# An SSM convolution with a 16-expert feed-forward on one core: the first convolution kernels computed on VectorE alone, the later ones tied to given heads

## The chip, the core and the metric

The kernel runs on one core of a Trainium2 chip. The core has a TensorE for matrix products, a VectorE (DVE in the profile) and a ScalarE (ACT) for element-wise work, a GpSimd (POOL), and a SyncE (SP) that here only issues DMA transfers. Sixteen DMA engines move data between DRAM and the on-chip memory. Each engine has its own instruction queue and takes it in order; engines wait for each other through semaphores. The metric is the device time of one execution in microseconds; lower is better.

## What is computed

The input `x` has 128 batch rows, 32 heads and 512 positions. Cut to what matters, the reference is:

```python
# per head: a convolution kernel from a diagonal state space model
K = 2 * einsum('hn,hnl->hl', Ct, exp(dtA[:, :, None] * arange(512))).real
y = causal_convolution(x, K) + x * D          # by FFT in the reference
y = y * (arange(512) < length[:, None])       # each batch row has its length
# per token (128 * 32 tokens of 512 values): mixture of experts
scores = sigmoid(y @ gate_w.T) + bias         # 16 experts, the best 4 weighted
out = sum over the 4 experts of w * (silu(y @ Wg.T) * (y @ Wu.T)) @ Wd.T
out = out + (silu(y @ Sg.T) * (y @ Su.T)) @ Sd.T     # shared expert
return x + out
```

## The kernel before, in words

The work runs in four stages. Everything up to the third is put in order by a scheduler that goes over the program with a priority by the order in which it was written and gives an idle engine the first instruction that is ready, so an engine may run ahead of the written order, but never out of the order in which the scheduler laid it down.

**Start.** SyncE loads the small parameters, then the first blocks of the transposed input (`load_xt`) and the shared expert's weights. GpSimd fills constants: `dsk` (line 127), `run_on` and `run_e` (223 to 228), `f_r` and `f_i` (290, 291), the masks and counters. The convolution kernels `K` are made in chunks of *pairs* of heads, `CHUNKS = ((0, 2), (2, 4), (6, 4), (10, 6))`: first pair and number of pairs, so the first chunk makes heads 0 to 3. For a chunk, `waves` (line 295) computes angle, sine, cosine and magnitude over a table of 48 columns for each pair: `reduce_angle` (line 242) is a chain of six VectorE instructions, `exp_parts` (line 250) one of twelve that depend on each other. `kernels` (line 367) multiplies these into two small factors, of which TensorE forms the products `pk` (line 394); VectorE adds the skip term into `krow` (line 402), which is written to a scratch tensor `kd` in DRAM. `kernel_strip` (line 413) reads it back, shifted by one for each partition, as the Toeplitz matrix `strip` of a block of four heads: 1 MB, for block 0 in four pieces of 256 KB. In `waves` and `kernels` half of the element-wise products are given to GpSimd (lines 309, 349 to 351, 374, 382, 386, 389).

Beside the kernels, VectorE ranks the batch rows by length (lines 430 to 512): `to_rank`, `to_row`, `within`, and what only later stages need (`by_rank`, `reach`, `k_u`, `unit_rows`).

**Convolution.** Eight blocks `tb` of four heads, `h = 4 * tb + q`. `convolve` (line 515) makes four products of 512, 384, 256 and 128 columns into `py` (line 520), VectorE masks them into `yb` (line 527), TensorE transposes by `to_rank` into `pt` (line 530), and ScalarE copies to `yT` in `store` (line 531). At heads 0, 2 and 5 (`chunk_at`) the program makes a further chunk of kernels, waves and products together; at the first head of a block it issues the strip of the block after. At a block's end `yb` goes to DRAM on ScalarE's queue, the block's gate scores are made (`gates`, `sums`), and after each second block `route` picks the experts on VectorE. GpSimd's queue issues copies of `x` to the output, DRAM to DRAM, 1 MB for a part of four heads, tied to the last head of a block: `COPIES = {2: (0,), 3: (1,), 4: (2,), 5: (3,), 6: (4, 5), 7: (6, 7)}`.

**Shared expert** (`unit_step`): eight units of 512 tokens; the results are added onto the output rows by indirect DMAs from GpSimd (line 953). In this stage the slots of the expert tiles are worked out as well, and the first seven experts' weights loaded. From here on the order is written out by hand.

**Expert tiles** (`turn_of`): about 134 tiles of 128 tokens each: gather, transpose, two layers of products (lines 1054 and 1080), and an indirect DMA that adds onto the output (line 1090).

Of the kernel before, what the change touches and what calls it, by code (L numbers as in the profile page):

```python
# [28 lines left out]
F32 = mybir.dt.float32  # L29
BF16 = mybir.dt.bfloat16  # L30
F16 = mybir.dt.float16
I32 = mybir.dt.int32
# [6 lines left out]
P = 128  # L39
# [4 lines left out]
HB = 4  # L44
# [10 lines left out]
ONE_HOTS = 8  # L55
AHEAD = 4
# [19 lines left out]
def ssm_moe_kernel(  # L76
# [50 lines left out]
    nc.gpsimd.memset(dsk, 0.0)  # L127
# [21 lines left out]
    def load_xt(tb):  # L149
        t = xp.tile([P, KT, HB, P], F32, tag="x", name=f"xt{tb}")  # L150
        nc.sync.dma_start(out=t, in_=x_t[tb])
        return t

# [69 lines left out]
    nc.gpsimd.memset(run_on, 1.0)  # L223
    nc.gpsimd.memset(run_on[:, :, 0:1], 0.0)

    run_e = const.tile([P, RB * HB, E], F32, tag="run_e", name="run_e")
    nc.gpsimd.memset(run_e, 1.0)
    nc.gpsimd.memset(run_e[:, :, 0:1], 0.0)

    def floor_div(out_, in_, by):  # L230

        nc.vector.tensor_scalar(
            out_, in_, 1.0 / by, -(by - 1) / (2.0 * by), ALU.mult, ALU.add
        )
        nc.vector.tensor_scalar(out_, out_, ROUND, None, ALU.add)
        nc.vector.tensor_scalar(out_, out_, ROUND, None, ALU.subtract)

# [35 lines left out]
    CHUNKS = ((0, 2), (2, 4), (6, 4), (10, 6))  # L273
# [16 lines left out]
    nc.gpsimd.memset(f_r, 0.0)  # L290
    nc.gpsimd.memset(f_i, 0.0)
# [3 lines left out]
    def waves(c0, n, lead):  # L295


        w = lead + n * NX
        v, r, k, q = (wide(t, w) for t in ("wv", "wr", "wk", "wq"))
        s, mag = wide("ws", w, I32), wide("wm", w)  # L300

        def pairs(t):
            return t[:, lead:].rearrange("p (c x) -> p c x", x=NX)

        by_l = lab.unsqueeze(1).to_broadcast([P, n, NX])
        nc.vector.tensor_mul(
            pairs(r), by_l, dta_i[:, c0 : c0 + n].unsqueeze(2).to_broadcast([P, n, NX])
        )
        nc.gpsimd.tensor_mul(
            pairs(v), by_l, dta_r[:, c0 : c0 + n].unsqueeze(2).to_broadcast([P, n, NX])  # L310
        )
        if lead:
            nc.vector.tensor_copy(r[:, :lead], dta_i)
            nc.vector.tensor_copy(v[:, :lead], dta_r)
        reduce_angle(r, k)
        nc.vector.scalar_tensor_tensor(k, r, -1.0, r, ALU.mult, ALU.max)
        nc.scalar.activation(k, k, AF.Sin, bias=half_pi, scale=-1.0)
        half = None
        if lead:
            half = ptile("half")  # L320
            nc.scalar.activation(half, r[:, :lead], AF.Sin, scale=0.5)
        nc.scalar.activation(r, r, AF.Sin)
        exp_parts(v, q, wide("we", w), s)
        s = s.bitcast(F32)
        nc.vector.scalar_tensor_tensor(mag, q, 1.0, s, ALU.add, ALU.mult)
        return tuple(pairs(t) for t in (mag, k, r)), (mag, q, s, r, half)
# [22 lines left out]
    nc.gpsimd.tensor_mul(m0, nar, nar)  # L349
    nc.gpsimd.tensor_mul(m1, aim, aim)  # L350
    nc.gpsimd.tensor_add(m0, m0, m1)
# [15 lines left out]
    def kernels(c0, n, mag, cos, sin):  # L367

        cs = slice(c0, c0 + n)

        for j in range(2):
            rows = slice(j * N, (j + 1) * N)
            nc.vector.tensor_mul(f_r[rows, cs, j, :], cos[rows, :, LA:], mag[rows, :, LA:])
            nc.gpsimd.tensor_mul(f_i[rows, cs, j, :], sin[rows, :, LA:], mag[rows, :, LA:])
# [7 lines left out]
        nc.gpsimd.tensor_mul(e_i, sin[:, :, :LA], mag[:, :, :LA])  # L382
# [3 lines left out]
        nc.gpsimd.tensor_mul(g_t, e_i, by_i)  # L386
        nc.vector.tensor_add(g_r, g_r, g_t)
        nc.vector.tensor_mul(g_i, e_r, by_i)
        nc.gpsimd.tensor_mul(e_i, e_i, by_r)
# [12 lines left out]
        nc.vector.tensor_add(  # L402
# [7 lines left out]
        for h in range(2 * c0, 2 * (c0 + n)):  # L410
            kd_of[h] = kd[h - 2 * c0 : h - 2 * c0 + 1, :]

    def kernel_strip(tb):
        s = ks1.tile([P, HB, L], F32, tag="strip", name=f"strip{tb}", bufs=2)

        each = 1 if tb == 0 else HB
        for q in range(0, HB, each):
            kd = kd_of[tb * HB + q]
            nc.sync.dma_start(
                out=s[:, q : q + each, :],  # L420
                in_=bass.AP(kd.tensor, kd.offset, [[1, P], [PAD + L, each], [1, L]]),
            )
        strip[tb] = s

    kernels(*CHUNKS[0], *first)
    kernel_strip(0)


    len_col = const.tile([P, 1], F32, tag="len_col", name="len_col")
    nc.vector.tensor_copy(len_col, len_col_i)  # L430
    key_row = const.tile([P, B], F32, tag="key_row", name="key_row")
    nc.vector.tensor_copy(key_row, len_row_i)
    key_col = const.tile([P, 1], F32, tag="key_col", name="key_col")
    for key, raw, own in ((key_row, key_row, cpos), (key_col, len_col, ppos)):
        nc.vector.tensor_scalar(key, raw, 0.0, float(L), ALU.max, ALU.min)
        if key is key_col:
            num_len = const.tile([P, 2], F16, tag="num_len", name="num_len")
            nc.vector.tensor_copy(num_len[:, 0:1], ppos)
            nc.vector.tensor_copy(num_len[:, 1:2], key)
        nc.vector.scalar_tensor_tensor(key, key, float(P), own, ALU.mult, ALU.subtract)  # L440
# [14 lines left out]
    to_rank_h = const.tile([P, P], F16, tag="to_rank_h", name="to_rank_h")  # L455
    nc.vector.tensor_copy(to_rank_h, to_rank)

    by_rank_ps = ps_m.tile([P, 2], F32, tag="m", name="by_rank_ps")
    nc.tensor.matmul(by_rank_ps, lhsT=to_rank_h, rhs=num_len, start=True, stop=True)
    by_rank = const.tile([P, 2], F32, tag="by_rank", name="by_rank")  # L460
    nc.vector.tensor_copy(by_rank, by_rank_ps)


    reach = const.tile([P, KT], BF16, tag="reach", name="reach")
    nc.vector.memset(reach, 1.0)
    for n in range(1, KT):
        nc.vector.tensor_scalar(
            reach[:, n : n + 1], by_rank[:, 1:2], float(n * P), None, ALU.is_gt
        )

    unit = const.tile([P, NU], BF16, tag="unit", name="unit")
    nc.vector.tensor_scalar(unit, upos, 0.0, None, ALU.is_equal)
    reach_sum = const.tile([P, 1], F32, tag="reach_sum", name="reach_sum")
    nc.vector.tensor_reduce(reach_sum, reach, AX.X, ALU.add)
    reach_b = const.tile([P, 1], BF16, tag="reach_b", name="reach_b")
    nc.vector.tensor_copy(reach_b, reach_sum)
    k_u_ps = ps_m.tile([1, NU], F32, tag="m", name="k_u_ps")
    nc.tensor.matmul(k_u_ps, lhsT=reach_b, rhs=unit, start=True, stop=True)
    k_u = const.tile([1, NU], I32, tag="k_u", name="k_u")
    nc.vector.tensor_copy(k_u, k_u_ps)  # L480


    div = const.tile([P, 2], F32, tag="div", name="div")
    mod = const.tile([P, 1], F32, tag="mod", name="mod")
    floor_div(div[:, 0:1], rank, UB)
    floor_div(div[:, 1:2], ppos, UB)
    nc.vector.scalar_tensor_tensor(mod, div[:, 0:1], -float(UB), rank, ALU.mult, ALU.add)
    same_mod = const.tile([P, P], F16, tag="same_mod", name="same_mod")
    nc.vector.tensor_scalar(same_mod, pmod, mod, None, ALU.is_equal)
    row_u = const.tile([P, NU], F16, tag="row_u", name="row_u")  # L490
    nc.vector.tensor_scalar(
        row_u, cpos[:, :NU], div[:, 0:1], ppos, ALU.is_equal, ALU.mult
    )
    row_ps = ps_m.tile([P, NU], F32, tag="m", name="row_ps")
    nc.tensor.matmul(row_ps, lhsT=same_mod, rhs=row_u, start=True, stop=True)
    part = const.tile([P, TU // P], F32, tag="part", name="part")
    nc.vector.tensor_scalar(
        part, cpos[:, : TU // P], float(P // UB), div[:, 1:2], ALU.mult, ALU.add
    )
    unit_rows = const.tile([P, NU, TU // P], I32, tag="unit_rows", name="unit_rows")  # L500
    nc.vector.scalar_tensor_tensor(
        unit_rows,
        row_ps.unsqueeze(2).to_broadcast([P, NU, TU // P]),
        float(H),
        part.unsqueeze(1).to_broadcast([P, NU, TU // P]),
        ALU.mult,
        ALU.add,
    )
# [3 lines left out]
    nc.vector.tensor_scalar(within, lpos, len_col, None, ALU.is_lt)  # L512
# [328 lines left out]
    def dep(of, on, why):  # L841
        tc.add_manual_dep(of.ins, on.ins.name, SYNC, reason=why)

# [4 lines left out]
    COPIES = {2: (0,), 3: (1,), 4: (2,), 5: (3,), 6: (4, 5), 7: (6, 7)}  # L848

    chunk_at = {0: CHUNKS[1], 2: CHUNKS[2], HB + 1: CHUNKS[3]}  # L850
    for tb in range(NB):
        yb = yp.tile([P, HB, L], F32, tag="yb", name=f"yb{tb}")
        x_next = load_xt(tb + 1) if tb + 1 < NB else None
        for q in range(HB):
            turned = convolve(tb, q, xb, yb)
            if tb * HB + q in chunk_at:
                c0, n = chunk_at[tb * HB + q]
                kernels(c0, n, *waves(c0, n, 0)[0])
            if q == 0 and tb + 1 < NB:
                kernel_strip(tb + 1)  # L860
# [355 lines left out]
```

## Time and profile before

| | us |
|---|---|
| time, median of 3 runs | 943.94 (941.65 to 944.29) |
| the profiled execution, its own time | 942.44 |
| its span, first to last instruction | 940.7 |

| stage of the profiled execution | from, us | to, us | TensorE busy, us |
|---|---|---|---|
| start, up to the first convolution product | 0 | 27.6 | 1.7 |
| convolution, 8 blocks | 27.6 | 146.3 | 109.0 |
| shared expert | 146.3 | 298.0 | 147.9 |
| expert tiles | 298.0 | 940.7 | 624.6 |

The stages are read from the timeline: the first product of line 520 starts at 27.59, the first of line 929 (shared expert) at 146.31, and the first of line 1054 (expert tiles) at 298.12. The busy time of each is taken from the windows by stage.

A row of the timeline gives start, duration, engine, line of the program, operation, the tiles it writes and reads, its shape and how many instructions were merged; in brackets stands how long its engine was idle before it and what released it. A row of the waits gives total time, number of times and the longest. `SPq` and `ACTq` are the instructions that issue DMA transfers on those engines.

### The profile page before, as it was taken

What the parts mean: (1) busy time and instruction counts of PE and PEld (TensorE: products, weight loads), DVE (VectorE), ACT (ScalarE), POOL (GpSimd) and SP (SyncE); (2) the same over time, 40 slices, a digit from 0 to 9 for tenths busy, and PEclk for the clock granted to TensorE, in tenths of its full rate; (3) what the DMA queues carried; (4) which work ended last, traced back from release to release, by engine and by line L of the source; (5) the groups of instructions that cost most, each with busy time, mean ns of one, the idle gap of its engine ahead of it and who ended that gap; (6) DMA issues with size and microseconds to landing.
All of it is one profiled execution on the core that took longest, in us unless ns stands there. A gap on an engine that the chain in (4) does not pass through costs nothing.

```text
span 940.7 us, 14509 instructions
## 1 busy us (share of the span) xinstructions
PE 883.1 (94%) x2960; PEld 442.0 (47%) x2960; DVE 409.3 (44%) x1406; ACT 190.0 (20%) x375; POOL 422.7 (45%) x376
## 2 busy tenths in 40 slices
PE   0799997999999999999999999999999999999993
PEld 0455553444544444454444444444444444444441
DVE  7954555486950233433343334333433233344331
ACT  0122221111222122211222122212211111222220
POOL 4210000222456455655565456645655545566553
PEclk9999999999999999999999999999999999999997
DMA  4378873276769756776577567756766556667664
GB/s 163 108 253 290 293 275 137 30 249 132 184 96 233 198 111 115 138 170 116 110 135 181 114 115 126 130 101 110 134 113 114 100 106 109 109 130 138 118 114 83
DMA packets 54673, 135.95 MB, mean 145 GB/s; under 512 B 12400, under 2 KB 12560, under 8 KB 50960
## 3 DMA queue, kind: packets, MB, share of 16 engines
q0 software_dynamic: 36256, 89.77, 50.6%
q1 hardware_dynamic: 14064, 36.15, 11.3%
q10 hardware_dynamic: 4224, 8.39, 2.3%
q8 instruction: 71, 1.16, 0.5%
q14 instruction: 58, 0.48, 0.1%
HBM read 288.08 MB, written 60.64 MB: 371 GB/s over the span
## 4 chain that ended last, share of the span: by engine, by line
PE 66%; issue 1%; SPq 0%; POOL 0%; DVE 0%; ACT 0%; POOLq 0%
PE g L1054 34%; PE o L1080 24%; PE m L1022 4%; PE u L1072 3%; PE o L944 1%; POOL out L1090 0%; SPq L1157 0%; POOL yg L894 0%; SPq L1105 0%; SPq L1140 0%; SPq L1141 0%; DVE zt L1066 0%; SPq L1142 0%; ACT sgt L1065 0%; SPq L880 0%
## 5 line engine op out<-in xcount | busy, mean ns | idle before, releaser
L1054 PE MATMUL g<-store,yt 128*128 x742 | 343.0, 596 | 1.8 <-issue 1.5
L1090 POOL DMA_INDIRECT out<-ob,put x134 | 211.3, 1577 | 242.6 <-DVE junk L1029 214.4
L1080 PE MATMUL o<-store,zT 128*128 x536 | 252.2, 593 | 0.1
L1066 DVE SCALAR_TENSOR_TENSOR zt<-g,wt,sgt 128x256 f32<-128x256 f32 x135 | 65.3, 484 | 306.7 <-ACT sgt L1065 306.7
L1054 PEld LDWEIGHTS g<-store,yt 128*128 128x128 f32 x742 | 130.3, 190 | 118.7 <-issue 117.4
L1080 PEld LDWEIGHTS o<-store,zT 128*128 128x128 f32 x536 | 101.4, 190 | 129.3 <-issue 124.6
L894 POOL DMA_INDIRECT yg<-y_rows,get x140 | 138.1, 987 | 42.7 <-issue 31.7
L1089 DVE COPY ob<-o 128x512 f32<-128x512 f32 x134 | 92.7, 692 | 109.7 <-PE o L1080 101.6
L1028 ACT COPY yt<-m 128x512 f32<-128x512 f32 x136 | 79.7, 586 | 227.7 <-PE m L1022 219.3
L1065 ACT ACTIVATE sgt<-g 128x256 f32<-128x256 f32 x135 | 51.9, 384 | 268.2 <-PE g L1054 267.4
L953 POOL DMA_INDIRECT out<-ob,unit_rows x32 | 50.2, 1568 | 98.8 <-ACT ob L951 93.1
L520 PE MATMUL py<-strip,xt 128*128 128x512 f32 (+3 forms) x256 | 79.0, 447 | 7.9 <-DMA strip<-kd 7.9
L1022 PEld LDWEIGHTS m<-ident,yg 128*128 128x128 f32 x373 | 48.6, 141 | 73.1 <-issue 73.0
L1022 PE MATMUL m<-ident,yg 128*128 128x128 f32 x373 | 63.1, 273 | 1.3 <-issue 1.0
L944 PE MATMUL o<-store,z 128*128 128x512 f32 x128 | 57.7, 597 | 1.2 <-ACT yt L1028 1.2
L1075 DVE COPY zT<-u 128x256 f32<-128x256 f32 x134 | 56.3, 420 | 0.7 <-PE u L1072 0.7
L520 PEld LDWEIGHTS py<-strip,xt 128*128 128x128 f32 x256 | 42.5, 195 | 25.3 <-issue 12.3
L1072 PE MATMUL u<-ident,zt 128*128 128x128 f32 x268 | 51.2, 273 | 0.6 <-DVE zt L1066 0.6
L929 PE MATMUL g<-store 128*128 128x512 f32 x92 | 43.0, 602 | 3.1 <-issue 2.5
L865 POOL DMA_DIRECT2D out<-in_x x8 | 4.4, 558 | 88.3 <-ACT store L531 88.3
L929 PE MATMUL u<-store 128*128 128x512 f32 x92 | 42.2, 593 | 0.0
L809 DVE TENSOR_SCALAR cols<-tpos_h,stl,tok 128x143 f16<-128x143 f16 x128 | 41.8, 331 | 0.0
(272 smaller groups left out, 499.0 us busy)
## 6 DMA issues: line engine op xcount, KB each, us to landing
store<-in_w_all SPq DMA_DIRECT2D x143, 1536.0 KB
xt<-in_x_t SPq DMA_DIRECT2D x8, 1024.0 KB
y_rows<-yb ACTq DMA_DIRECT2D x8, 1024.0 KB
out<-in_x POOLq DMA_DIRECT2D x8, 1024.0 KB, 9.0
strip<-kd SPq DMA_DIRECT2D x7, 1024.0 KB
yg<-y_rows,get POOLq DMA_INDIRECT x140, 4.3
out<-ob,put POOLq DMA_INDIRECT x134, 4.8
strip<-kd SPq DMA_DIRECT2D x4, 256.0 KB
```

The lines of the kernel that those rows point to most:

```text
L520: nc.tensor.matmul(py[:, : L - jt * P], lhsT=xt[:, jt, q, :], rhs=strip[tb][:, q, jt * P :], start=(jt == 0), stop=(jt == KT - 1),)
L894: nc.gpsimd.indirect_dma_start(out=at(yg, t), out_offset=None, in_=y_rows[:, :], in_offset=bass.IndirectOffsetOnAxis(ap=made["get"][:, t : ...
L929: nc.tensor.matmul(ps[it], lhsT=w_sh[:, c0 : c0 + P], rhs=yT[:, u, kt, :, :].rearrange("p h b -> p (h b)"), start=(kt == KT - n), stop=(kt ...
L944: nc.tensor.matmul(po, lhsT=at(zu, u)[:, it, q * P : (q + 1) * P], rhs=w_sh[:, c0 : c0 + L], start=(it == 0), stop=(it == IT - 1),)
L1022: nc.tensor.transpose(pt[:, q, :], at(yg, t)[:, q * P : (q + 1) * P], ident)
L1028: nc.scalar.copy(at(yt, t), pt)
L1054: mm = nc.tensor.matmul(pgu, lhsT=at(yt, t)[:, q, :], rhs=ring_flat[:, bass.ds(w0s[t] + q * 2 * I, 2 * I)], start=(q == KT - n), stop=(q = ...
L1066: nc.vector.scalar_tensor_tensor(at(zs, t), pgu[:, I:], at(wts, t), sg, ALU.mult, ALU.mult)
L1072: nc.tensor.transpose(at(p_z, t)[:, it, :], at(zs, t)[:, it * P : (it + 1) * P], ident)
L1080: mm = nc.tensor.matmul(po, lhsT=at(zts, t)[:, it, :], rhs=ring_flat[:, bass.ds(w0s[t] + WD + it * L, L)], start=(it == 0), stop=(it == IT ...
L1089: nc.vector.tensor_copy(ob, po)
L1090: add = nc.gpsimd.indirect_dma_start(out=out, out_offset=bass.IndirectOffsetOnAxis(ap=made["put"][:, t : t + 1], axis=0), in_=ob, in_offse ...
```

## The change

Six edits belong together.

1. The fills of `dsk`, `run_on`, `run_e`, `f_r` and `f_i` go from GpSimd to VectorE.
2. For the first chunk, the products that GpSimd made in `waves` and `kernels`, and the three of lines 349 to 351, go to VectorE. Later chunks keep them on GpSimd.
3. A helper `behind` ties an instruction to the first chunk's `krow`. It is put on the first instructions of the ranking, on `within`, and on the first instruction of later chunks' waves on both engines. What else ranks and only serves later stages moves into a function `ranks`, called when block 2 begins.
4. `keep_warm` puts 16 TensorE products of bf16 ones, 128x512 each, behind the first chunk's `krow`.
5. The chunks become five, and waves and products are written at different heads; a strip is issued as soon as its chunk is made, and no earlier than one block ahead.
6. The copies of `x` begin one block later, and four of the eight are issued behind the last block.

```diff
-    nc.gpsimd.memset(dsk, 0.0)
+    nc.vector.memset(dsk, 0.0)
...
-    nc.gpsimd.memset(f_r, 0.0)
-    nc.gpsimd.memset(f_i, 0.0)
+    nc.vector.memset(f_r, 0.0)
+    nc.vector.memset(f_i, 0.0)
...
-    CHUNKS = ((0, 2), (2, 4), (6, 4), (10, 6))
+    CHUNKS = ((0, 2), (2, 2), (4, 4), (8, 4), (12, 4))
...
-        nc.vector.tensor_mul(
+        first_op = nc.vector.tensor_mul(
             pairs(r), by_l, dta_i[...]
         )
-        nc.gpsimd.tensor_mul(
+        if c0:
+            behind(first_op)
+        first_op = (nc.gpsimd if c0 else nc.vector).tensor_mul(
             pairs(v), by_l, dta_r[...]
         )
+        if c0:
+            behind(first_op)
...
+        other = nc.gpsimd if c0 else nc.vector
...
-            nc.gpsimd.tensor_mul(f_i[rows, cs, j, :], sin[rows, :, LA:], mag[rows, :, LA:])
+            other.tensor_mul(f_i[rows, cs, j, :], sin[rows, :, LA:], mag[rows, :, LA:])
...
-    kernels(*CHUNKS[0], *first)
+    def keep_warm(on):
+        warm = ps_u.tile([P, KT, P], F32, tag="u", name="warm")
+        for n in range(WARM):                      # WARM = 16
+            mm = nc.tensor.matmul(
+                warm,
+                lhsT=ones,
+                rhs=ones.unsqueeze(1).to_broadcast([P, KT, P]),
+                start=True,
+                stop=True,
+            )
+            dep(mm, on, "behind the first kernels")
+
+    chunk0 = kernels(*CHUNKS[0], *first)
     kernel_strip(0)
+    keep_warm(chunk0)
+
+    def behind(op):
+        dep(op, chunk0, "later in VectorE's order")
...
-    COPIES = {2: (0,), 3: (1,), 4: (2,), 5: (3,), 6: (4, 5), 7: (6, 7)}
-    chunk_at = {0: CHUNKS[1], 2: CHUNKS[2], HB + 1: CHUNKS[3]}
+    COPIES = {3: (0,), 4: (1,), 5: (2,), 6: (3,), 7: (4, 5, 6, 7)}
+    waves_at = {0: CHUNKS[1], 2: CHUNKS[2], 7: CHUNKS[3], 12: CHUNKS[4]}
+    kernels_at = {0: CHUNKS[1], 5: CHUNKS[2], 10: CHUNKS[3], 16: CHUNKS[4]}
+    made_waves, strips = {}, [1]
     for tb in range(NB):
+        if tb == 2:
+            by_rank, reach, k_u, unit_rows = ranks()
...
             turned = convolve(tb, q, xb, yb)
-            if tb * HB + q in chunk_at:
-                c0, n = chunk_at[tb * HB + q]
-                kernels(c0, n, *waves(c0, n, 0)[0])
-            if q == 0 and tb + 1 < NB:
-                kernel_strip(tb + 1)
+            h = tb * HB + q
+            if h in waves_at:
+                made_waves[waves_at[h]] = waves(*waves_at[h], 0)[0]
+            if h in kernels_at:
+                kernels(*kernels_at[h], *made_waves[kernels_at[h]])
+            if strips[-1] in (tb, tb + 1) and strips[-1] < NB and strips[-1] * HB in kd_of:
+                kernel_strip(strips[-1])
+                strips.append(strips[-1] + 1)
```

## The prediction

> **What bounds the kernel now.** I first read the page's engine table and its slices, then the windows by stage, then TensorE's waits, and last the timeline of the first 50 us. The page:
>
> ```profile
> PE 883.1 (94%) x2960; PEld 442.0 (47%) x2960; DVE 409.3 (44%) x1406; ACT 190.0 (20%) x375; POOL 422.7 (45%) x376
> ...
> PE   0799997999999999999999999999999999999993
> ```
>
> TensorE is busy all the time but for the first slice (23.5 us each) and a little of the second and seventh. The expert stages, from 146.3 us on, have TensorE as their limit (772.5 us busy in 794.4 us), and the change touches nothing in them. So only two things can move the end: when the first convolution product starts (27.59 us), and what TensorE idles between it and 146.3 us: 118.7 us with 109.0 busy, 9.7 idle. The waits of TensorE in that stage say who causes that (total us, times, longest):
>
> ```profile
> PE py L520 <- DMA strip<-kd: 7.9, 4, 5.0
> PE pt L530 <- DVE yb L527: 3.9, 4, 1.3
> PE g L929 <- issue: 1.7, 1, 1.7
> ```
>
> The 5.0 is the wait that ends at 27.59; 2.9 us are three later waits for a strip, 3.1 of the 3.9 us lie in the first 60 us. The chain that ends at 27.59, by the timeline:
>
> ```profile
> 4.11 0.69 DVE L254 TENSOR_SCALAR logs<-logs 128x32 f32<-128x32 f32 x1 [3.16 <-DMA logs<-in_log_a]
> 5.04 1.73 DVE L256 TENSOR_SCALAR dn_k<-dn_k 128x32 f32<-128x32 f32 x1
> 5.06 0.51 POOL L223 MEMSET run_on<- 128x512 f32 x1
> 8.88 0.18 DVE L270 SCALAR_TENSOR_TENSOR dn<-dn_q,dn_s 128x32 f32<-128x32 f32 x1
> 10.50 0.25 DVE L306 TENSOR_TENSOR wr<-lab,dta_i 128x96 f32<-128x96 f32 x1
> 12.69 0.22 DVE L254 TENSOR_SCALAR wv<-wv 128x112 f32<-128x112 f32 x1
> 16.53 0.27 DVE L325 SCALAR_TENSOR_TENSOR wm<-wq,ws 128x112 f32<-128x112 f32 x1
> 20.47 0.17 DVE L362 SCALAR_TENSOR_TENSOR ct_i<-t,rd 128x16 f32<-128x16 f32 x1
> 22.62 0.21 DVE L402 TENSOR_TENSOR krow<-pk,dsk 32x64 f32<-32x64 f32 x1
> 24.26 1.76 SPq L419 DMA_DIRECT2D strip<-kd  x4
> 27.59 4.50 PE L520 MATMUL py<-strip,xt 128*128 128x512 f32 x8 [5.01 <-DMA strip<-kd]
> ```
>
> Up to `krow` (22.83) it is VectorE, which is never idle for long there; then 4.76 us of DRAM write, read back and first wait. Call the end of `krow` K.
>
> **The fills and first products (edits 1 to 3): K comes earlier.** I go through the chain. (a) `dn`, 13 dependent instructions of 32 columns, took 4.95 us (4.11 to 9.06). Five of line 261 in a row take 1.09 us, so 0.21 each is its pace; two stand out, 0.69 and 1.73 us, while GpSimd fills. GpSimd without fills (0.51 us each for four, 0.41 for the small ones) is done at some 4.5 instead of 6.9. The chain then takes 0.4 + 12 x 0.21 = 3.0: done at 7.1, gain 2.0. (b) From there to `wr` at 10.75 lie 1.7 us, mostly ranking; `dta`, two copies and `wr` need 0.7: done at 7.8, gain 2.95. (c) Angle chain 10.86 to 12.78, exponent chain 12.69 to 16.80: one after the other 6.0 us. Both start from data that is ready at the same time, and dependent instructions leave gaps (0.33 us apart at 0.19 us of issue), so they can be interleaved: 4.9 us then; sequential, 13.8. I take 13.0: gain 3.8. (d) The factors `ct` took 3.84 us with five instructions of the next chunk between (0.9), a 0.50 us line 332 that is 0.17 elsewhere (0.3) and two of the ranking (0.2); added are six small products from GpSimd (0.75). 3.2 us: 16.2. (e) The last six products, two of them with a round trip to GpSimd, 1.36 us; on one engine 1.1: 17.3. (f) `pk` and `krow` 0.83: K = 18.1, gain 4.7.
>
> The fills land on VectorE, which has no row of a 512-column fill; they cost at most five times GpSimd's 0.51 = 2.6 us, and VectorE is idle for 3.16 us up to 4.11, so nothing if the scheduler puts them there, 2.6 if it doesn't; below nothing is excluded, the instructions only come on top. The idle gap takes them: nothing. The large loads that fill the DMA engines end at 17.2 us (share 1.04 in 16 to 17, 0.18 in 17 to 18), so the write at 18.1 meets empty engines; K earlier than 17 would be worth less.
>
> **The warm products (edit 4).** In the first head TensorE is slow: eight instructions take 4.50 us, in a later block
>
> ```profile
> 87.03 2.32 PE L520 MATMUL py<-strip,xt 128*128 128x384 f32 x8
> ```
>
> The weight loads are 0.86 us apart at the start and 0.43 in the shared expert for the same 512 columns: half speed, until some 31.7 us, 4.1 us after the first product. (The granted clock reads 1.00 in all these windows and does not show it.) An f32 instruction of 512 columns makes two passes in 0.43, so a bf16 one is an estimated 0.215 us at full and 0.43 at half speed. By this row's 4.1 us, 9.5 of the 16 are slow: 4.1 + 6.5 x 0.215 = 5.5 us. The Trainium skill ("TensorE: Matmul & The Clock Gate", Part 1, on the clock gate) says that the slow stretch is some 3.4 us of time, not a number of products, and falls differently from run to run: 8 slow, 5.1 us. K to the first product is 4.76 us, so the warm products overrun by 0.3 to 0.8 us: I take 0.6, nearer the row. In return the first head runs at full speed: 4.50 - 2.32, some 2.1 us. The first product then starts at 18.1 + 4.76 + 0.6 = 23.5, gain 4.1.
>
> **The chunks (edit 5): the strips become late.** What a strip takes is seen at block 1:
>
> ```profile
> 34.93 0.27 DVE L402 TENSOR_TENSOR krow<-pk,dsk 32x128 f32<-32x128 f32 x1
> 36.77 0.38 SPq L419 DMA_DIRECT2D strip<-kd  x1
> ```
>
> 1.84 us from `krow` to issue; the DMA share is up until 41.6, so 4.9 us to land with the engines otherwise idle, 6.7 in all from `krow`. *Strip 1:* before, its chunk began at 16.5 beside the first; now it may not begin before K. Angle 2.3, exponent 4.1, products 2.3, ranking between 1.2, `pk` and `krow` 1.2: K + 11.1, landed at K + 17.8. Block 1 wants it after four heads of 2.81 us (yb to yb in a quiet stretch) and 0.35 for `pk`: K + 5.4 + 11.6 = K + 17.0. A stall of 0.8; ends nothing and 3.4 (ranking all ahead of it). *Strip 2:* its products stand behind head 5 now, so `krow` comes some 1.4 us after head 5's products (as in the second chunk before, 16 small products in 0.62 us and 0.3), the strip is issued at +3.4 and lands at +8.3. Head 8 follows after heads 6 and 7 and part of the gates: +6.6. A stall of 1.7; ends nothing and 4. Behind that product TensorE's whole queue waits. *Strips 3 to 7* are issued where they were. For 3.1 us of waits for `yb` early on (VectorE busy with 192- and 288-column waves ahead of it) the smaller chunks and later ones leave 0.8: gain 2.3; ends 0 and 3.1.
>
> `ranks` brings some 25 VectorE instructions of 0.15 us and three small TensorE products into blocks 2 and 3, beside `route` (10 us of VectorE in 13): 0.3 us on TensorE, and 0.5 for waits in its order (`cw_ps` waits 0.3 us in the same place); ends nothing and 2. Queued behind such a wait are the products of the next head.
>
> **The copies of x (edit 6).** Before, strip waits of 0.2, 1.2 and 1.5 us come at blocks 4, 5 and 7, with the strip issued 14 us ahead and DMA shares of 0.8 to 1.0:
>
> ```profile
> 85.92 0.39 SPq L419 DMA_DIRECT2D strip<-kd  x1
> ...
> 100.00 1.10 PE L520 MATMUL py<-strip,xt 128*128 128x512 f32 x2 [1.21 <-DMA strip<-kd]
> ```
>
> Block 3 loses its copy (gain 0.2), blocks 4 to 6 keep one. Four at the end instead of two: each pair was done by 152 us; from 155 to 180 the engines are idle (share under 0.15), and the first indirect add that needs them comes at 180.5. Nothing, with 20 us of cover; GpSimd has no other work queued behind the four issues (0.52 us each).
>
> **The sum**, from the profiled execution's own 942.44: start -4.1, warm clock -2.1, `yb` waits -2.3, strips 1 and 2 +2.5, `ranks` +0.8, copies -0.2: -5.4, or 937.0. The median of the runs shown is 1.5 above the profiled execution; I carry that over: **938.5 us**.
>
> **Rivals.** *Strips in time* (0.18): the scheduler runs chunk 1 and chunk 2 ahead on idle VectorE, as it did before with the chunk of head 5, whose waves began at 35.9, in head 1. No 2.5: 936.0, and 934 with (c) fully interleaved and copies easing strips 5 and 7. *Given back* (0.18): stalls at their upper ends, 3.4 + 4 instead of 2.5, take 4.9: 943.4. This is no change. *Slower* (0.14), one mechanism: strip 2 now follows block 1's `xt` and block 0's output, 2 MB that are still moving when it is issued. Under a full load a strip needs 14 us instead of 4.9, as strip 5 shows; then block 2 waits 9.1 more: 938.5 + 9.1 = 947.6. It decides from about 10.3 us on from issue to landing (4.9 + 5.4). Against it: at head 4 both loads are issued and need 6 us, which is before the strip. That the change does nothing, because TensorE is busy 94%, is excluded: its start depends on K.
>
> **Numbers.** Forecast 0.50, the rest as given. A difference of 0.3%, 2.8 us, is about what can be told from no change. Faster: forecast and the first rival, 0.68; same 0.18; slower 0.14. The forecast's own range is 936 to 941.5; 8 in 10 need 933.5 to 944.5, which leaves out the slow rival.
>
> **What would show it.** `krow` ending near 18.1, GpSimd's fills gone from 5 to 7 us, the line 256 instruction back near 0.2; the first product near 23.5 with weight loads 0.43 apart from the start; waits for strips at the first heads of blocks 1 and 2 of about 0.8 and 1.7; the shared expert starting near 141 and the rest shifted whole. Wrong it would be if the warm products hold back the ranking's two products in TensorE's queue, so that VectorE stands behind `rank` with chunk 1 behind it, or if the strips wait far longer.

## The result, and the profile after

The changed kernel takes 935.58 us, the median of 4 runs (933.84 to 936.54); the kernel before, run beside it, 942.80 (940.97 to 944.29). The ratio is 0.9919, with a 95% interval of 0.9900 to 0.9938: faster by 7.2 us. The forecast was 938.5, with a range of its own of 936 to 941.5, which the result misses by 0.4 us, and eight chances in ten for 933.5 to 944.5, in which it lies. The profiled execution took 936.54 us with a span of 934.8, 5.9 less than before.

The page of the changed kernel, its engine table and the slices of TensorE: the first slice is no longer empty, the rest is all but as before.

```profile
PE 887.1 (95%) x2976; PEld 444.1 (48%) x2976; DVE 411.9 (44%) x1452; ACT 190.2 (20%) x377; POOL 419.8 (45%) x366
...
PE   2999979999999999999999999999999999999993
```

Then the chain to the first convolution product, from the timeline of the changed kernel (start, duration, engine, line, operation). (Its line 553 is 520 before, 560 is 527, 563 is 530, 404 is 394, 412 is 402, 430 is 419, and 440 are the warm products.)

```profile
4.59 0.25 DVE L261 TENSOR_SCALAR dn_k<-dn_k 128x32 f32<-128x32 f32 x1
...
6.89 0.19 DVE L275 SCALAR_TENSOR_TENSOR dn<-dn_q,dn_s 128x32 f32<-128x32 f32 x1
...
7.91 0.20 DVE L311 TENSOR_TENSOR wr<-lab,dta_i 128x96 f32<-128x96 f32 x1
...
8.31 0.21 DVE L259 TENSOR_SCALAR wv<-wv 128x112 f32<-128x112 f32 x1
...
12.03 0.28 DVE L334 SCALAR_TENSOR_TENSOR wm<-wq,ws 128x112 f32<-128x112 f32 x1
...
15.15 0.17 DVE L371 SCALAR_TENSOR_TENSOR ct_i<-t,rd 128x16 f32<-128x16 f32 x1
...
16.91 0.21 DVE L412 TENSOR_TENSOR krow<-pk,dsk 32x64 f32<-32x64 f32 x1 [0.62 <-PE pk L404]
...
17.27 4.71 PE L440 MATMUL warm<-ones 128*128 128x512 bf16 x16 [0.40 <-DVE krow L412]
...
17.53 1.34 SPq L418 DMA_DIRECT2D kd<-zero  x4
...
19.37 1.76 SPq L430 DMA_DIRECT2D strip<-kd  x4
...
22.66 2.39 PE L553 MATMUL py<-strip,xt 128*128 128x512 f32 x8 [0.60 <-DMA strip<-kd]
```

`krow` ends at 17.12 instead of 22.83, and the first head's eight instructions take 2.39 us instead of 4.50. The fills on VectorE lie in its idle time ahead of the chain, from 0.99 to 3.27 us. From the end of `krow` to the first product it is 5.54 us, 0.78 more than before: four writes of zeros (1.34 us of issue) now stand in SyncE's queue between the write of `krow` and the first strip.

The waits of TensorE in its first 150 us (total us, times, longest):

```profile
PE pt L563 <- DVE yb L560: 3.2, 4, 1.5
PE py L553 <- DMA strip<-kd: 2.8, 3, 1.5
PE g L967 <- issue: 1.7, 1, 1.7
```

0.6 of the 2.8 us is the wait at 22.66, the rest are two waits from block 4 on. Blocks 1 and 2 do not wait for their strips. The windows by stage of the changed kernel (stretch; its length; busy time and instructions of TensorE, its weight loads, VectorE, ScalarE, GpSimd; granted clock; DMA share, GB/s):

```profile
22.66:138.64 115.98, 107.01 (x569) 66.23 (x570) 76.01 (x274) 25.89 (x49) 14.13 (x31) 1.00 0.70 234
138.64:292.39 153.75, 149.81 (x471) 69.81 (x471) 93.10 (x384) 30.46 (x52) 53.19 (x37) 0.99 0.67 158
292.39:934.80 642.41, 624.61 (x1913) 305.52 (x1911) 223.55 (x671) 131.28 (x271) 347.69 (x271) 0.99 0.67 125
```

| stage | before, us | after, us | difference |
|---|---|---|---|
| start | 27.59 | 22.66 | -4.93 |
| convolution | 118.72 (109.0 busy) | 115.98 (107.0 busy) | -2.74 |
| shared expert | 151.65 | 153.75 | +2.10 |
| expert tiles, to the end of the span | 642.74 | 642.41 | -0.33 |

In the kernel before, the first product of the expert tiles starts at 297.96 us; the table takes that.

The loss in the shared expert lies in its first eight products, which the change does not touch. They are, before and after:

```profile
146.31 3.69 PE L929 MATMUL g<-store 128*128 128x512 f32 x8 [1.68 <-issue]
...
138.64 5.39 PE L967 MATMUL g<-store 128*128 128x512 f32 x8 [1.67 <-issue]
```

The windows of the changed kernel show that the clock was lowered (the last three columns are granted clock, DMA share and GB/s):

```profile
138.00:139.00 1.00, 0.36 (x1) 0.30 (x2) 0.00 (x0) 0.00 (x0) 0.18 (x1) 0.99 0.94 193
...
140.00:141.00 1.00, 1.00 (x2) 0.34 (x1) 0.00 (x0) 0.00 (x0) 0.00 (x0) 0.50 1.00 401
...
143.00:144.00 1.00, 1.00 (x5) 0.51 (x4) 0.00 (x0) 0.00 (x0) 0.00 (x0) 1.00 1.08 369
```

From 139 to about 142.4 the clock is granted at 0.50, after TensorE had waited 0.9, 0.7 and 1.7 us within five. These waits alone do not decide it. The kernel before has the same three (0.87, 0.68 and 1.68 us), and so, within 0.2 us, do eight of the experiments below, all those without extra products in this place; in each of these nine profiles the eight products take 3.69 us. What else decides was not found. Two of the four executions, this one among them, have a mean clock of 0.992 and take 936.3 and 936.5 us, the others 0.994 and 0.995 and 933.8 and 934.9, and 22 executions of the kernel before fall into the same two groups (seven of 943.8 to 944.9, fifteen of 941.2 to 943.4); that all of them lost their time in this place is not shown. The profile of before, with 0.994, stands against one with 0.992, so the profiles make the gain smaller (5.9) than the medians do (7.2).

### The profile page after: what moved, and what is told of

The parts are those of the page before. It is cut to its first block, busy times and chain, and to the rows that moved or that the text cites. A ratio compares the mean times of both kernels' runs of the same rounds, so it can differ in the third digit from the quotient of the medians.

```text
span 934.8 us, 14577 instructions
## 1 busy us (share of the span) xinstructions
PE 887.1 (95%) x2976; PEld 444.1 (48%) x2976; DVE 411.9 (44%) x1452; ACT 190.2 (20%) x377; POOL 419.8 (45%) x366
## 4 chain that ended last, share of the span: by engine, by line
PE 67%; issue 1%; SPq 0%; POOL 0%; DVE 0%; ACT 0%; POOLq 0%; DVEq 0%
PE g L1092 34%; PE o L1118 24%; PE m L1060 4%; PE u L1110 3%; PE o L982 1%; POOL out L1128 0%; SPq L1195 0%; POOL yg L932 0%; SPq L1143 0%; DVE zt L1104 0%; SPq L1178 0%; SPq L1179 0%; SPq L1180 0%; ACT sgt L1103 0%; DVE zT L1113 0%
## 5 line engine op out<-in xcount | busy, mean ns | idle before, releaser
L553 PE MATMUL py<-strip,xt 128*128 128x512 f32 (+3 forms) x256 | 76.8, 437 | 2.8 <-DMA strip<-kd 2.8
L553 PEld LDWEIGHTS py<-strip,xt 128*128 128x128 f32 x256 | 42.1, 191 | 19.5 <-issue 11.1
```

The source lines that it names most:

```text
L553: nc.tensor.matmul(py[:, : L - jt * P], lhsT=xt[:, jt, q, :], rhs=strip[tb][:, q, jt * P :], start=(jt == 0), stop=(jt == KT - 1),)
```

## The experiments

All times are medians; "end of `krow`" and the start of the shared expert are read from each kernel's timeline. The kernel before took 942.5, 943.85 and 941.81 us beside the three batches.

### One part of the change undone

**The warm products left out.**

```diff
-    keep_warm(chunk0)
```

> The changed kernel without the 16 warm products. If the half-speed clock is what they remove: krow ends at 17.1 as before, the first convolution product still starts near 22.7 (the strip sets that, not the warm products, which end at 22.0), but its eight instructions take some 4.3 us instead of 2.4, and the shared expert starts 1.6 to 2.1 us later than in the changed kernel (138.6): time near 937.5. Rival: the slow first head is swallowed by the waits for yb and strips that follow it; then the shared expert starts within 0.5 us and the time stays near 935.6.

940.98 us, ratio to before 0.9980 (0.9970 to 0.9991): three quarters of the gain are gone, more than either theory gave. The first head takes 4.22 us as expected. But the shared expert starts at 144.25, 5.6 us late. The scheduler, with other work on TensorE, had put the third chunk's products behind the first part of head 6 (44.66 instead of 42.75); strip 2 is issued at 47.83 instead of 45.35, and block 2 waits, as TensorE's timeline of this kernel shows:

```profile
54.44 3.33 PE L552 MATMUL py<-strip,xt 128*128 128x512 f32 x4 [2.73 <-DMA strip<-kd]
```

The windows there (the last three columns are granted clock, DMA share and GB/s):

```profile
52.00:56.00 4.00, 1.56 (x2) 0.84 (x3) 3.40 (x11) 0.93 (x3) 1.88 (x5) 0.67 0.99 349
56.00:60.00 4.00, 4.00 (x12) 0.98 (x11) 0.32 (x2) 0.30 (x1) 0.29 (x1) 0.50 1.03 401
```

The wait is 2.73 us, and behind it the clock is 0.50 until about 60: four instructions that take some 1.5 us at full speed (2.39 for eight, and some overlap) take 3.33.

**The four old chunks.**

```diff
-    CHUNKS = ((0, 2), (2, 2), (4, 4), (8, 4), (12, 4))
+    CHUNKS = ((0, 2), (2, 4), (6, 4), (10, 6))
...
-    waves_at = {0: CHUNKS[1], 2: CHUNKS[2], 7: CHUNKS[3], 12: CHUNKS[4]}
-    kernels_at = {0: CHUNKS[1], 5: CHUNKS[2], 10: CHUNKS[3], 16: CHUNKS[4]}
+    chunk_at = {0: CHUNKS[1], 2: CHUNKS[2], HB + 1: CHUNKS[3]}
...
+            if h in chunk_at:
+                c0, n = chunk_at[h]
+                kernels(c0, n, *waves(c0, n, 0)[0])
```

> The changed kernel with the four chunks, the heads and the strips of the kernel before. If the five chunks bring next to nothing (the trace shows no wait for strip 1 or 2, and 2.9 us of early waits on VectorE and ScalarE against 3.1 before): shared expert within 1 us of 138.6, time 934.5 to 936.5. By the prediction's step, undoing it removes strip waits of 2.5 us and brings back 2.3 us of waits for yb: also near no change, but with both waits changed in the trace. Rival: the smaller chunks are what lets the early start reach the end; then block 1 waits for its strip by 3 us or more, and the time is 938.5 or above.

939.3 us, the median of eleven executions (a twelfth took 5164 us and is left out, as it is in the ratio), ratio 0.9973 (0.9958 to 0.9988). The rival is right about the time and the place, not about the size of the wait. With the ties a chunk of four pairs cannot start beside the first one: its products wait 1.3 us for VectorE, strip 1 is issued at 32.69 instead of 28.35, block 1 waits 1.5 us for it, and the granted clock is 0.77 and 0.81 in the windows from 36 to 44.

**The old places of the copies.**

```diff
-    COPIES = {3: (0,), 4: (1,), 5: (2,), 6: (3,), 7: (4, 5, 6, 7)}
+    COPIES = {2: (0,), 3: (1,), 4: (2,), 5: (3,), 6: (4, 5), 7: (6, 7)}
```

> The changed kernel with the copies of x where they were. If the copies matter only for the later strips: waits for strips from block 3 on go from 2.3 back to some 2.9 us, time +0.6, near 936.2, and the four copies at the end cost nothing now, so nothing is won by two. Rival: the copies fill the DMA engines in blocks 2 to 6 and are half of the stage's gain of 2.7 us: waits for strips of 3.7 us or more, time +1.4 or more, 937.

935.84 us, ratio 0.9931 (0.9917 to 0.9946), not to be told from the changed kernel; the later strip waits are 2.4 us against 2.3. As made, this edit brings nothing that can be measured.

**The fills, the products and the ties, each undone,** one execution each, read for the end of the first `krow`. First all seven fills:

```diff
-    nc.vector.memset(f_r, 0.0)
-    nc.vector.memset(f_i, 0.0)
+    nc.gpsimd.memset(f_r, 0.0)
+    nc.gpsimd.memset(f_i, 0.0)
...
```

> The changed kernel with the fills of dsk, run_on, run_e, f_r and f_i back on GpSimd; read for the end of the first krow alone (17.1 in the changed kernel), since the scheduler then puts the third chunk's products behind a part of head 6 and strip 2 comes late again. By the prediction's step (a) the fills on GpSimd cost the chain up to dn 2.0 us: krow at 19.1, dn at 9.1 with two instructions of 0.7 and 1.7 us. Rival: with less else on GpSimd and VectorE the fills hide: krow within 0.5 us of 17.1.

19.13, so 2.0 us, with the same long instruction as before:

```profile
5.04 1.73 DVE L261 TENSOR_SCALAR dn_k<-dn_k 128x32 f32<-128x32 f32 x1
...
18.92 0.21 DVE L412 TENSOR_TENSOR krow<-pk,dsk 32x64 f32<-32x64 f32 x1 [0.69 <-PE pk L404]
```

Then the products:

```diff
-        first_op = (nc.gpsimd if c0 else nc.vector).tensor_mul(
+        first_op = nc.gpsimd.tensor_mul(
...
-        other = nc.gpsimd if c0 else nc.vector
+        other = nc.gpsimd
```

> The changed kernel with the first chunk's products back on GpSimd; read for the end of the first krow alone. By steps (c) to (e) the two exponent and angle chains were one after the other because one input came from GpSimd, and the last products made two round trips: krow 1.0 to 2.5 us later, 18.1 to 19.6. Rival: the chains are interleaved all the same and the shared work saves VectorE's time: krow within 0.5 us.

17.26, 0.14 us later: the rival. The exponent chain ends at 12.36, within 0.1 us of the changed kernel (12.31), with its input from GpSimd. Last, the ties:

```diff
-        dep(op, chunk0, "later in VectorE's order")
+        return op
```

> The changed kernel without the ties behind the first krow; read for the end of the first krow alone. By steps (b) and (d) ranking and the next chunk's first instructions stood between: 1.0 + 1.4 us, krow at 18.5 to 19.5. Rival: they only fill gaps between dependent instructions: krow within 0.5 us.

20.01, so 2.9 us, more than both steps together. `dn` ends 1.2 us later, the exponent chain 2.5, the factors 2.8. Ahead of `dn` it is not the ranking's work that costs most but a wait: one of its inputs comes by DMA, and the whole queue of VectorE stands behind it.

```profile
7.71 0.23 DVE L461 CAST key_row<-len_row_i 128x128 f32<-128x128 int32 x1 [1.07 <-DMA len_row_i<-in_length]
...
10.20 0.21 DVE L249 TENSOR_SCALAR wk<-wr 128x112 f32<-128x112 f32 x1
10.33 0.21 DVE L259 TENSOR_SCALAR wv<-wv 128x112 f32<-128x112 f32 x1
```

The last two lines are the first of the angle chain and of the exponent chain: without the ties, too, the two chains alternate.

The whole times of these three (943.0, 938.9, 942.1) are single executions, and all three hold a wait for strip 2 as well (3.0, 2.9 and 2.3 us). What each of the three edits is worth in the whole time is not shown.

### How much strip 2 has to spare

**Its products one head later.**

```diff
-    kernels_at = {0: CHUNKS[1], 5: CHUNKS[2], 10: CHUNKS[3], 16: CHUNKS[4]}
+    kernels_at = {0: CHUNKS[1], 6: CHUNKS[2], 10: CHUNKS[3], 16: CHUNKS[4]}
```

> The changed kernel with the products of the third chunk (heads 8 to 15) written behind head 6 instead of head 5, so that TensorE makes them after head 6's own products, one head (2.8 us) later. In the changed kernel strip 2 is issued at 45.35 and its transfers fill the engines up to some 50.5; block 2 begins at 50.85, so its slack is some 0.3 us. If that is so: TensorE waits 2 to 3 us for strip 2, and since it has then been idle the clock falls to half for 3 to 7 us behind it, as in the run without warm products: 4 to 6 us more, near 940. Rival: the slack is larger (the wait for ScalarE just ahead hides it) and the clock stays: within 1 us of the changed kernel, 935 to 936.5.

944.85 us, ratio 1.0014 (1.0004 to 1.0023): the whole gain is gone, and the time is slightly above that of the kernel before. The wait is twice what was expected, by TensorE's waits from 60 to 100 us:

```profile
PE py L553 <- DMA strip<-kd: 5.6, 1, 5.6
```

The timeline of SyncE's queue shows what it waits behind:

```profile
49.62 0.33 SPq L152 DMA_DIRECT2D xt<-in_x_t  x1
50.06 0.93 SPq L430 DMA_DIRECT2D strip<-kd  x2
```

`xt` and both strips 2 and 3 are issued within 1.4 us, 3 MB; the strip that is wanted first lands some 10.4 us after its issue (TensorE's wait ends at 60.41), against 5 when it goes alone. The clock is at 0.50 from 57 to 63.

**Its products two heads earlier, without warm products.**

```diff
-    kernels_at = {0: CHUNKS[1], 5: CHUNKS[2], 10: CHUNKS[3], 16: CHUNKS[4]}
+    kernels_at = {0: CHUNKS[1], 3: CHUNKS[2], 10: CHUNKS[3], 16: CHUNKS[4]}
...
-    keep_warm(chunk0)
```

> Without the warm products, and with the third chunk's products written behind head 3, so that TensorE makes them in head 4. The run without warm products was 5.4 us slower than the changed kernel, of which the slow first head is 1.3 to 1.8. If the rest came from strip 2 (its products stood behind the first part of head 6, strip wait 2.7 us, then half clock): that wait is gone here, no half clock after the first head, shared expert near 140.3, time 937 to 938. Rival: the warm products themselves are worth 5 us (the order of VectorE or the clock of the first block needs them): 940 or above.

933.90 us, ratio 0.9898 (0.9879 to 0.9916), 3 to 4 us better than expected. Without the warm products this is no slower than the changed kernel, and some 7 us faster than the same kernel with the products behind head 5. The wait in block 2 is gone (from 40 to 100 us TensorE waits 0.2 us for strips), and behind the first head the clock is 1.00 in all windows up to 68. So most of what the kernel loses without the warm products is the late strip 2 and not the half-speed head.

### Further than the change

**Warm products ahead of the shared expert as well.**

```diff
         xb = x_next
+    keep_warm(parts_last[0], 10)
     conv.close()
```

> The changed kernel with 10 more warm products behind the last gate scores, in the gap of 1.7 us before the shared expert. In the changed kernel's profile the granted clock is 0.50 from 139 to 142.5 and the first eight products of the shared expert take 5.4 us instead of 3.7; two of its four executions have a mean clock of 0.992 and are 2 us longer than those with 0.994 and 0.995. If the gap is what lets the clock fall: first eight products 3.7 us, every execution at 0.994 or more, median 1 to 2 us lower, near 934. Rival: the products stand ahead of the shared expert's in TensorE's queue and delay them by up to 2.2 us, or the clock falls anyway: 935.5 to 938.

934.98 us, 934.03 to 935.25 in six executions with clocks of 0.993 to 0.995; ratio 0.9919 (0.9906 to 0.9932). The eight products take 3.60 us. The executions of 936 us are gone, as the first theory has it, though six executions are few to show it; the median moves too little to be told from the changed kernel's four runs.

**Both: warm products there, and the third chunk's products behind head 3.**

> The changed kernel with the 10 warm products ahead of the shared expert and the third chunk's products behind head 3. If strip 2 just makes it in the changed kernel, the earlier issue wins nothing by itself, at most the 0.2 us wait for strip 2: 934.0 to 935.3, with all executions within 1.5 us. Rival: the products now stand ahead of VectorE's factors, TensorE waits for them in block 1 by 1 to 3 us: 936 to 938.

932.18 us (931.97 to 933.27), ratio 0.9882 (0.9866 to 0.9897): better than expected. The last `yb` comes at 131.34 instead of 133.77, 2.4 us earlier, though the changed kernel has no strip wait in blocks 1 and 2 that could go. Most of it is in other waits: the early ones are 1.4 us against 2.9, and those for later strips 1.8 against 2.3. From the first convolution product to 60 us only this one is left:

```profile
36.45 0.63 PE L563 MATMUL pt<-to_rank,yb 128*128 128x128 f32 x4 [1.42 <-DVE yb L560]
```

The kernel with the products behind head 3 and no warm products has its last `yb` at 132.95; so the first warm products are worth 1.6 us here.

**The zeros ahead of `krow`.**

```diff
+    for c0, n in CHUNKS:
+        kds[c0] = d1.tile([2 * n, L + PAD], F32, tag=f"kd{c0}", name=f"kd{c0}")
+        nc.sync.dma_start(out=kds[c0][:, L:], in_=zero[: 2 * n, :])
...
+                if last_product:
+                    dep(mm, last_product.pop(), "behind the head's products")
```

> As the last, and the five small writes of zeros behind the kernels' rows are issued at the start, ahead of the first krow; the second chunk's products are tied behind the first head's, so that their order stays. In the changed kernel four of these writes (1.34 us of issue) stand between the first krow's write and the first strip, and 2.2 us pass from the one issue to the other, 1.4 before. If they hold the strip back: first strip issued 0.5 to 0.8 us earlier, near 18.6 to 18.9; the first product can then only start as early as the warm products end (21.9 to 23.2), so 0 to 0.7 us are won: 933.5 to 935. Rival: the end of the large loads at 17.2 us holds the write of krow back: the first strip is issued near 19.3 all the same.

935.02 us, ratio 0.9910 (0.9896 to 0.9923), 2.8 us worse than the kernel with both edits, on which it is built. The first strip is issued 1.41 us behind the write of `krow`, as before the change, so the zeros did hold it back. Nothing is won, since the first product then waits for the warm ones (22.93), and the scheduler's order elsewhere changed: 2.9 us of waits for `yb` up to 40 us, strip 2 issued at 46.78 and 1.3 us late.

**All copies behind the last block.**

```diff
-    COPIES = {3: (0,), 4: (1,), 5: (2,), 6: (3,), 7: (4, 5, 6, 7)}
+    COPIES = {7: tuple(range(NB))}
```

> The version with early products of the third chunk and warm products ahead of the shared expert, with all eight copies of x behind the last block. If the copies are what keeps the engines full in blocks 3 to 7: the waits for strips there (0.5 and 1.3 us) go, the shared expert starts near 134.9, and the eight copies, at the pace of the four now (done by 150), are done near 163, ahead of the first indirect add at some 170: 930 to 931. Rival: strip, input and output alone keep the waits, or the first adds wait for the copies and with them the queue of GpSimd: 932 or above.

930.66 us (929.93 to 931.33), ratio 0.9876 (0.9859 to 0.9892), the lowest time of all these kernels, 4.9 us below the changed kernel's (4.0 by the ratios). It too is built on the kernel with both edits. No wait for a strip is left from block 1 on. The view of all that touches `x` in DRAM says when the copies land (min, median, max from issue):

```profile
L903 POOL DMA_DIRECT2D out<-in_x x8: 515/518/769, 132.9 to 136.7; - x8
...
DMA to landing us min/median/max: 8.9/17.4/26.8
```

The last is issued at 136.7 and the slowest takes 26.8, so all have landed by 163.5; the first indirect add comes at 169.78. Against the version with four copies kept in the blocks (932.18, in another batch) it is 1.5 us less, but the intervals of the two ratios overlap: which of the two is better is not shown.

## Why the prediction was right, point by point

| term of the sum, us | forecast | measured |
|---|---|---|
| end of `krow` | -4.7 | -5.71 |
| from there to the first product | +0.6 | +0.78 |
| first head at full clock | -2.1 | -2.11 in the head, 1.6 at the last `yb` |
| waits for `yb` | -2.3 | -0.2 |
| strips 1 and 2 | +2.5 | 0 |
| `ranks` | +0.8 | no wait seen |
| copies, later strips | -0.2 | -0.6, not confirmed by the experiment |
| shared expert | 0 | +2.1 |
| sum, on the profiled execution | -5.4 | -5.9 |

The measured terms, read one at a time, add up to -5.7. The total came out right in part by luck: against the forecast, strips 1 and 2 are 2.5 us better, the end of `krow` 1.0 and `ranks` 0.8, and the waits for `yb` and the shared expert 2.1 us worse each. What happened is nearer to the rival *Strips in time*, which left out the 2.5, said 936.0, or 934 with the two chains of step (c) fully interleaved, and had a chance of 0.18; strips 1 and 2 were in time, the chains do alternate, and the median is 935.58. Its reason, chunks that run ahead on an idle VectorE, is only part of it, as the part on the strips shows.

**The start is right and too small by 1.0 us.** Step (a), fills against VectorE, is shown: 2.0 forecast, 2.0 measured. Steps (b) to (d), where other work leaves VectorE, were 2.4 together (4.4 less 2.0); the ties measure 2.9. Of these, 1.2 lie ahead of `dn`, where the prediction had only the fills; most of that is the wait for `len_row_i`. The interleaving of step (c) belongs to neither edit alone: the chains alternate without the ties, and with the products back on GpSimd. In the kernel before, which has neither edit, they are one after the other; which of the two would do was left open. Moving the first products to VectorE brings next to nothing by itself, 0.14 us. The three undone one at a time make 5.0 of 5.7 us, and 0.7 is accounted for by none of them alone.

**The lag behind `krow` has the right size and half the reason.** In the profiled execution the zeros in SyncE's queue held the strip, not the warm products, which ended at 21.98. In most later kernels it was the warm products, and the first product waits for no strip. The estimate of 0.43 and 0.215 us for each is borne out by their weight loads, 0.43 apart up to 19.36 and then 0.21:

```profile
18.93 0.15 PEld L440 LDWEIGHTS <-ones 128*128 128x128 bf16 x1 [0.28 <-issue]
19.36 0.15 PEld L440 LDWEIGHTS <-ones 128*128 128x128 bf16 x1 [0.28 <-issue]
19.66 1.82 PEld L440 LDWEIGHTS <-ones 128*128 128x128 bf16 x9 [0.15 <-issue]
```

The 16 took 4.7 to 6.2 us in the kernels that have them. The Trainium skill ("TensorE: Matmul & The Clock Gate", Part 1) says that the slow stretch falls differently from run to run, and this spread agrees with that; both estimates, 5.1 from the skill's 3.4 us and 5.5 from the row, lie in it. The sign that the prediction gave for being wrong came halfway: the ranking's two products stand behind the warm ones, from 18.8, when their input is ready, to 21.8. But VectorE had chunk 1 to work on and did not wait for them.

**Strips 1 and 2 are where the prediction failed, with errors of both signs.** For strip 1 the chunk took less than forecast: its `krow` ends 9.7 us behind the first one's, not 11.1, the strip has landed by 33.1 us, 16.0 behind instead of 17.8, and block 1 begins at 33.8, 16.7 behind. The need was about right (17.0), the stall of 0.8 did not come. For strip 2, issue and landing were about right (3.4 and 8.3 us behind head 5, though the terms given, 1.4 and 1.84, make 3.2 for the issue). Measured are 3.4 and some 8.0: the strip's megabyte has been moved by 50.0 us. The step that failed is the time of need, "head 8 follows after heads 6 and 7 and part of the gates: +6.6". Head 8 starts 8.9 us behind head 5. The changed kernel's timelines have the issue of the strip on SyncE's queue,

```profile
45.35 0.37 SPq L430 DMA_DIRECT2D strip<-kd  x1
```

and on TensorE two waits and head 8 itself:

```profile
47.94 0.63 PE L563 MATMUL pt<-to_rank,yb 128*128 128x128 f32 x4 [0.20 <-DVE yb L560]
...
50.39 0.63 PE L563 MATMUL pt<-to_rank,yb 128*128 128x128 f32 x4 [0.54 <-ACT wr L331]
50.85 2.32 PE L553 MATMUL py<-strip,xt 128*128 128x512 f32 x8
```

Two heads of 2.81 us leave 1.0 of the 6.6 for the gates. The products of two chunks are missing in it: those of the third, which stand behind head 5 themselves (0.6), and those of the fourth, which ran ahead (0.7). Two waits of 0.20 and 0.54 us come on top. Even without these waits head 8 would start at 50.1, just behind the strip; so what took the stall away is mostly TensorE's own work, and the slack is some 0.8 us.

The gain for `yb` failed too: 3.1 us of early waits became 2.9, of other heads, for VectorE and once for ScalarE. The two errors, +2.5 and -2.1, cancel, and that is luck. What the strips cost was shown by the experiments instead: a head later, 5.6 us of wait and no gain left. That is the mechanism of the slow rival, with a landing of 10.4 us where it was to decide at 10.3. The changed kernel was one head away from it.

**`ranks` and the copies** are hidden, as said: in TensorE's waits no product of the moved ranking appears, and the experiment on the copies shows no difference. Of the copies' rival reading, that they are what fills the engines, the last experiment shows a part: with all of them moved the strip waits from block 4 on go.

**Not foreseen** was that a wait of TensorE can cost twice, the wait and a half clock behind it. It moved the shared expert by 2.1 us in the profiled execution and made the experiments' losses larger than their waits. Which of the scheduler's choices made the early waits for `yb` stay, and why the third chunk behind head 3 takes half of them away, was not taken apart further.

## What to carry to other kernels

When a long stage has to wait for a first result, count what the engine that makes it does for others before it, and what it waits for on their behalf: here tying independent work behind it brought 2.9 us and keeping GpSimd's fills from running beside VectorE's chain 2.0, while moving its last products onto VectorE brought 0.1. A transfer that arrives just in time can only get worse by a little delay. Move its producer ahead until it has slack: here the producer one head later took the whole gain away, and two heads earlier replaced the warm products. To find the time of need, count everything that lies between, the products of other chunks too. Then add a half clock to a wait of TensorE like the 2.7 and 5.6 us here.

## What the runs showed of the hardware

A VectorE instruction on 128x32 values takes 1.73 us beside GpSimd's large fills, in two kernels, and 0.25 us in the changed one, where a fill of 8x128 runs beside it; the same fill takes 0.48 us on VectorE and 0.51 on GpSimd.

TensorE's clock fell to one half behind waits that left it partly busy: 0.9 and 2.7 us in block 2 without warm products, 0.9 and 1.5 ahead of block 1 with the old chunks, 5.6 with the late products, and 0.9, 0.7 and 1.7 within five at the shared expert, where nine other profiles with the same waits kept the full clock. It fell 1.3 to 2.0 us after the last of these waits had begun. By windows of 1 us it stayed low for 3.4 us (shared expert, old chunks) or for 6.8 (the other two), so for one or two of the same stretch.

The granted clock reads 1.00 in the first windows of the profiles looked at, although the first products run at half speed; there the distance of the weight loads, 0.86 against 0.43 us, is the only sign.
